# Gate and up of an expert as a 2 by 2 block product with seven block products for eight

## Chip, cores and metric

The kernel runs on one core of a Trainium2 chip. The metric is device time in microseconds (us) of one execution. "Expert phase" below means the part of the program in which the sixteen experts of the mixture of experts are computed one after another; "offset" is time counted from the first matmul of an expert.

## What is computed

The program has two layers: a convolution-like cross attention over 8 sequences of 256 tokens, then a mixture of experts with a shared expert. The change touches only the gated half of an expert:

```python
E, K, I = (16, 4, 352)          # experts, experts per token, hidden features
CAP = 256                       # token slots of an expert
xg = xpad[buf]                                            # (16, 256, 512)
gact = jax.nn.silu(jnp.einsum('ech,ehi->eci', xg, w_gate))
mid = gact * jnp.einsum('ech,ehi->eci', xg, w_up)
eout = jnp.einsum('eci,eih->ech', mid, w_down) * wbuf[..., None]
y = zeros.at[buf].add(eout)                               # scatter-add to tokens
```

For one expert, gate and up are two products of a 512 by 352 weight with 512 by 256 token columns, everything in float32.

## The kernel before

**Layout.** Features lie on the 128 partitions. The contraction of 512 is four chunks of 128. The 352 hidden features are two whole tiles of 128 (`NW = 2`) and a tail of 96. `w` holds gate and up of one expert as `[128, 2, 4, 352]`, `wd` the down weight, `xgT` the token columns as `[128, 4, 256]`, `mid` the result of gate times up.

**One expert** (loop at the end of the function). `gate_up` first does the tail: eight matmuls of 64 columns (L1046) and four of 128 (L1054, weights repacked into `wt` by `pack`), with two activations on L1063, one on L1067 and their multiplications by VectorE on L1064 and L1068. Then, for each of the two whole tiles, four matmuls for gate and four for up with 256 token columns (L1034), one Silu by ScalarE (L1041) and one multiplication by VectorE (L1042). After that `pack` copies the next expert's tail weights (ScalarE, L1017), `tokens` makes the next expert's `xgT` (VectorE: two column copies L1003, two transposes L404, both from the transferred `gb`), `find` computes the row numbers for the expert three ahead (sixteen small bf16 matmuls on L920 and VectorE's L928 to L943) and `gather` fetches those rows (GpSimd, indirect DMA, L977). `down` runs once for each half of the 256 tokens: three contraction tiles of 512 columns (L1080, the tail of `mid` first), a scaling by VectorE (L1088), and a scatter with addition into `out` by GpSimd (L1090, L1091). Then `compare` prepares the expert four ahead (VectorE, L907).

**Order.** The program order on every engine is the order in which the code is written; each engine works through its own list in order. Scatters of an expert wait for those of the expert before. The two scatters of expert 0 also wait for one another; from expert 1 on they do not.

**Transfers.** SyncE issues, for the expert three ahead, four weight loads (L859 to L864), then `slots` from the gathered rows (L989), then four loads of `gb` from `slots` (L992). Each of these waits in SyncE's list for the one before it to be issued, and `slots` and `gb` also for their data. There are three buffers for expert weights.

**Last experts.** Expert 15 has code of its own: it computes the two halves of the tokens one after the other, with matmuls of 128 token columns. There is nothing to gather or find for the last three.

**Room.** `xnT` holds the normalised tokens for the shared expert, 8192 floats a partition. Its last reader is the shared expert's last block, before expert 0. PSUM has two buffers of `ps_mm`, two of `ps_tr`, one of `ps_sm` and three of `ps_ex`; in the expert phase before the change only the last four are used.

Of the kernel before, what the change touches and what calls it, by code (L numbers as in the profile page):

```python
# [8 lines left out]
F32 = mybir.dt.float32  # L9
BF16 = mybir.dt.bfloat16  # L10
I32 = mybir.dt.int32
AF = mybir.ActivationFunctionType
# [8 lines left out]
P = 128  # L21
# [9 lines left out]
E, K, CAP, I, IS = 16, 4, 256, 352, 704  # L31
NSL = CAP // P
# [21 lines left out]
def ssm_attention__then__moe_kernel(  # L54
# [22 lines left out]
    nc = tc.nc  # L77
# [8 lines left out]
    ps_mm = ctx.enter_context(tc.tile_pool(name="ps_mm", bufs=2, space=PSUM))  # L86
    ps_tr = ctx.enter_context(tc.tile_pool(name="ps_tr", bufs=2, space=PSUM))
# [15 lines left out]
    xnT = keep.tile([P, NC, NT, P], F32, name="xnT")  # L103
# [156 lines left out]
    with ExitStack() as att:  # L260
# [591 lines left out]
    def load_expert(e):  # L852
# [92 lines left out]
    experts = {e: load_expert(e) for e in range(AHEAD)}  # L945
# [52 lines left out]
    def tokens(e):  # L998

        gb, g = moved.pop(e), gathered.pop(e)  # L1000
        wg = ffn.tile([P, NSL], F32, name="wg")
        for n in range(NSL):
            nc.vector.tensor_copy(wg[:, n : n + 1], g[:, n, L + e : L + e + 1])  # L1003
        xgT = ffn.tile([P, NC, CAP], F32, name="xgT")
        for n in range(NSL):
            transpose_blocks(xgT[:, :, n * P : (n + 1) * P], gb[:, n * NB : (n + 1) * NB])
        return xgT, wg

    NW, Q = I // P, P // 4
# [13 lines left out]
    def gate_up(xgT, mid, w, wt, cols, fs=(I // P, *range(I // P))):  # L1023

        halves = range(cols.start // P, cols.stop // P)
        for f in fs:
            pgu = ps_ex.tile([P, 2, CAP], F32, name="pgu", tag="ex")
            act = ffn.tile([P, CAP], F32, name="eact")  # L1030
            if f < NW:
                for k in range(2):
                    for c in range(NC):
                        nc.tensor.matmul(  # L1034
                            pgu[:, k, cols],
                            lhsT=w[:, k, c, f * P : (f + 1) * P],
                            rhs=xgT[:, c, cols],
                            start=(c == 0),
                            stop=(c == NC - 1),
                        )  # L1040
                nc.scalar.activation(act[:, cols], pgu[:, 0, cols], AF.Silu)  # L1041
                nc.vector.tensor_mul(mid[:, f, cols], act[:, cols], pgu[:, 1, cols])  # L1042
                continue
            for c in range(NC):
                for n in halves:
                    nc.tensor.matmul(  # L1046
                        pgu[2 * Q * n : 2 * Q * (n + 1), 1, 0:P],
                        lhsT=wt[:, c, P:],
                        rhs=xgT[:, c, n * P : (n + 1) * P],
                        start=(c == 0),  # L1050
                        stop=(c == NC - 1),
                    )
            for c in range(NC):
                nc.tensor.matmul(  # L1054
                    pgu[:, 0, cols],
                    lhsT=wt[:, c, 0:P],
                    rhs=xgT[:, c, cols],
                    start=(c == 0),
                    stop=(c == NC - 1),
                )  # L1060
            for n in halves:
                p, sl = 2 * Q * n, slice(n * P, (n + 1) * P)
                nc.scalar.activation(act[2 * Q : 3 * Q, sl], pgu[p : p + Q, 1, 0:P], AF.Silu)  # L1063
                nc.vector.tensor_mul(  # L1064
                    mid[2 * Q : 3 * Q, f, sl], act[2 * Q : 3 * Q, sl], pgu[p + Q : p + 2 * Q, 1, 0:P]
                )
            nc.scalar.activation(act[0 : 2 * Q, cols], pgu[0 : 2 * Q, 0, cols], AF.Silu)  # L1067
            nc.vector.tensor_mul(  # L1068
                mid[0 : 2 * Q, f, cols], act[0 : 2 * Q, cols], pgu[2 * Q : P, 0, cols]
            )  # L1070

    scattered = []
    between = route.tile([P, 1], F32, name="between")
    SYNC = mybir.DependencyInfo(mybir.DependencyClass.Sync, mybir.DependencyReason.DATA)

    def down(e, n, mid, wd, wg):
        po = ps_ex.tile([P, L], F32, name="eo", tag="ex")
        for k, f in enumerate((NW, *range(NW))):
            m = min(P, I - f * P)
            nc.tensor.matmul(  # L1080
                po,
                lhsT=mid[:m, f, n * P : (n + 1) * P],
                rhs=wd[:m, f, :],
                start=(k == 0),
                stop=(k == NW),
            )
        o = ffn.tile([P, L], F32, name="eo_sb", bufs=3)
        nc.vector.tensor_scalar_mul(o, po, wg[:, n : n + 1])  # L1088

        nc.gpsimd.memset(between, 0.0)  # L1090
        done = nc.gpsimd.indirect_dma_start(  # L1091
            out=out,
            out_offset=bass.IndirectOffsetOnAxis(ap=idx[:, e, n : n + 1], axis=0),
            in_=o,
            in_offset=None,
            compute_op=ALU.add,
        )


        done = done.ins  # L1100
        scattered.append(done)
        if e > 0:
            if n == 1:
                tc.declare_no_dep(done, scattered[2 * e], reason="other rows of out")
            for before in scattered[2 * (e - 1) : 2 * e]:
                tc.add_manual_dep(done, before.name, SYNC, reason="scatter")
# [6 lines left out]
    xgT_next = tokens(0)  # L1113
# [5 lines left out]
    for e in range(E):  # L1119
        w, wd = experts.pop(e)  # L1120
        wt = wt_next
        xgT, wg = xgT_next
        mid = ffn.tile([P, NI, CAP], F32, name="mid")
        if e + 1 < E:
            gate_up(xgT, mid, w, wt, slice(0, CAP))
            wt_next = pack(experts[e + 1][0])
            xgT_next = tokens(e + 1)
            if e + AHEAD < E:
                find(e + AHEAD, hots.pop(e + AHEAD))
                gathered[e + AHEAD] = gather(e + AHEAD)  # L1130
            for n in range(NSL):
                down(e, n, mid, wd, wg)
            if e + AHEAD + 1 < E:
                hots[e + AHEAD + 1] = compare(e + AHEAD + 1)
        else:

            gate_up(xgT, mid, w, wt, slice(0, P))
            gate_up(xgT, mid, w, wt, slice(P, CAP), (NW,))
            down(e, 0, mid, wd, wg)
            gate_up(xgT, mid, w, wt, slice(P, CAP), range(NW))  # L1140
            down(e, 1, mid, wd, wg)
        if e + AHEAD < E:
            experts[e + AHEAD] = load_expert(e + AHEAD)
            moved[e + AHEAD] = shuffle(gathered[e + AHEAD])
# [38 lines left out]
```

## Time and profile before

| | |
|---|---|
| time, median of 3 runs (lowest to highest) | 678.43 us (678.39 to 678.44) |
| profiled execution, its own time | 678.52 us |
| its span in the trace | 676.8 us |
| granted TensorE clock, mean | 0.995 |
| busy TensorE / VectorE / ScalarE / GpSimd | 654.2 / 385.8 / 184.2 / 320.2 us |
| expert 0 starts, expert 15 starts, last matmul ends | 419.3, 650.7, about 667 us |
| one expert, from 1 to 12 | 15.5 us |

Names: PE is TensorE's matmuls, PEld its weight loads, DVE VectorE, ACT ScalarE, POOL GpSimd, SP SyncE. A float32 matmul of the code appears in the trace as two instructions. Rows of the chain and of the timeline begin with start and length in us; `x32` counts merged instructions; in brackets stands the idle time before and what ended it. Rows of groups give count, busy us and the mean ns of one. Instructions of one engine overlap a little at their edges, so a recorded length can exceed the spacing between starts.

### The profile page before, as it was taken

The page shows a single profiled execution, that of the slowest core. Times are in us where ns is not written, and L with a number is a line of the kernel's source. Part 1 is how long each engine was busy: PE and PEld are TensorE (multiplying, and loading weights), DVE is VectorE, ACT ScalarE, POOL GpSimd, SP SyncE. Part 2 cuts the span into 40 slices and gives each one's busy share as a digit, 9 for nine tenths or more (in the row PEclk, how much of TensorE's full clock was granted, in tenths as well). Part 3 has the DMA queues.
Part 4 walks back from the last instruction along what each step waited for, and adds up shares of the span by engine and source line. Part 5 has one row for each costly group of instructions (what it writes and reads, how often), then busy time and mean ns, then how long its engine had stood idle before and what let it go on. Part 6 is the DMA issues. An engine that isn't in the chain of part 4 may idle for free.

```text
span 676.8 us, 9807 instructions
## 1 busy us (share of the span) xinstructions
PE 654.2 (97%) x3321; PEld 486.9 (72%) x3321; DVE 385.8 (57%) x932; ACT 184.2 (27%) x465; POOL 320.2 (47%) x509
## 2 busy tenths in 40 slices
PE   6899999998999999999999999999999999999994
PEld 5687877777867877876867685777776667777772
DVE  4956576878877776767536621444445545553231
ACT  2464533444342343313332010111121111111110
POOL 5677646877685777547120320243333444443111
PEclk9999999999999999999999999999999999999998
DMA  5793455555557536351008672588888889999822
GB/s 131 237 269 105 125 151 145 145 140 140 147 141 188 134 94 161 103 133 46 16 23 298 198 234 64 169 267 255 259 269 269 256 258 270 271 266 273 248 32 31
DMA packets 98439, 117.79 MB, mean 174 GB/s; under 512 B 11268, under 2 KB 64356, under 8 KB 98389
## 3 DMA queue, kind: packets, MB, share of 16 engines
q1 hardware_dynamic: 90932, 99.86, 48.9%
q0 software_dynamic: 7168, 17.04, 12.1%
q10 hardware_dynamic: 288, 0.26, 0.3%
q8 instruction: 26, 0.43, 0.3%
q14 instruction: 25, 0.20, 0.1%
HBM read 84.25 MB, written 32.88 MB: 173 GB/s over the span
## 4 chain that ended last, share of the span: by engine, by line
PE 85%; DVE 4%; DMA 3%; issue 2%; POOL 2%; ACT 2%; SPq 1%; POOLq 0%; DVEq 0%; ACTq 0%
PE sgu L168 20%; PE pgu L1034 15%; PE y L468 15%; PE eo L1080 12%; PE so L185 11%; PE pgu L1054 4%; PE pgu L1046 2%; PE sgt L154 2%; PE shared L468 2%; PE ip L920 1%; PE pt L529 1%; POOL kv L445 1%; DMA xs<-in_x 1%; DMA out<-eo_sb,idx 1%; DVE y L517 1%
## 5 line engine op out<-in xcount | busy, mean ns | idle before, releaser
L468 PE MATMUL y<-kv,toep 128*128 128x288 f32 x528 | 138.7, 407 | 4.8 <-DVE f L518 3.0
L468 PEld LDWEIGHTS y<-kv,toep 128*128 128x128 f32 x528 | 98.9, 190 | 35.4 <-issue 7.1
L977 POOL DMA_INDIRECT g<-xw_d,ido x32 | 34.9, 1092 | 170.8 <-DVE idx L943 132.3
L520 POOL TENSOR_TENSOR f<-f 128x256 f32<-128x256 f32 x60 | 43.8, 730 | 90.2 <-DVE f L518 85.0
L445 POOL TENSOR_TENSOR kv<-k 128x256 f32<-128x256 f32 x126 | 85.1, 707 | 0.0
L1091 POOL DMA_INDIRECT out<-eo_sb,idx x32 | 59.5, 1859 | 46.1 <-DVE eo_sb L1088 35.4
L168 PE MATMUL sgu<-xnT,swg 128*128 128x256 f32 (+1 forms) x400 | 78.1, 338 | 0.4 <-DVE tail L162 0.4
L1034 PE MATMUL pgu<-xgT,w 128*128 128x256 f32 (+1 forms) x384 | 78.2, 362 | 0.0
L168 PE MATMUL sgu<-xnT,swu 128*128 128x256 f32 (+1 forms) x400 | 77.9, 338 | 0.0
L1034 PEld LDWEIGHTS pgu<-xgT,w 128*128 128x128 f32 x384 | 68.2, 190 | 8.7 <-issue 0.5
L185 PE MATMUL so<-swd,smid 128*128 128x512 f32 x160 | 73.9, 593 | 0.0
L168 PEld LDWEIGHTS sgu<-xnT,swg 128*128 128x128 f32 x400 | 65.3, 191 | 7.9 <-DVE tail L162 0.6
L168 PEld LDWEIGHTS sgu<-xnT,swu 128*128 128x128 f32 x400 | 64.6, 191 | 6.3
L1080 PE MATMUL eo<-wd,mid 96*128 96x512 f32 (+1 forms) x132 | 59.4, 598 | 0.0
L1042 DVE TENSOR_TENSOR mid<-eact,pgu 128x256 f32<-128x256 f32 (+1 forms) x34 | 13.8, 406 | 77.6 <-ACT eact L1041 77.6
L491 DVE TENSOR_TENSOR y<-y,again 128x576 f32<-128x576 f32 x28 | 21.4, 766 | 57.8 <-PE y L468 48.1
L185 PEld LDWEIGHTS so<-swd,smid 128*128 128x128 f32 x160 | 29.9, 190 | 31.9 <-issue 30.4
L177 ACT ACTIVATE act<-sgu 128x256 f32<-128x256 f32 (+1 forms) x50 | 17.1, 341 | 121.6 <-PE sgu L168 121.6
L518 DVE TENSOR_TENSOR f<-y,z 128x512 f32<-128x512 f32 x64 | 44.3, 692 | 6.6 <-DVE y L517 0.5
L517 DVE TENSOR_TENSOR y<-y,q 128x512 f32<-128x512 f32 x64 | 44.8, 700 | 2.2
L1063 ACT ACTIVATE eact<-pgu 32x128 f32<-32x128 f32 x32 | 8.5, 267 | 129.0 <-PE pgu L1054 123.8
L1080 PEld LDWEIGHTS eo<-wd,mid 96*128 96x128 f32 (+1 forms) x132 | 24.1, 189 | 26.0 <-issue 23.5
(178 smaller groups left out, 928.2 us busy)
## 6 DMA issues: line engine op xcount, KB each, us to landing
toep<-win_d SPq DMA_DIRECT2D x28, 320.0 KB
slots<-g SPq DMA_DIRECT2D x16, 512.0 KB
gb<-slots SPq DMA_DIRECT2D x64, 128.0 KB
w<-in_L_ffn_w_gate SPq DMA_DIRECT2D x11, 704.0 KB
w<-in_L_ffn_w_up SPq DMA_DIRECT2D x11, 704.0 KB
got<-sent SPq DMA_DIRECT2D x26, 256.0 KB
wd<-in_L_ffn_w_down SPq DMA_DIRECT2D x11, 512.0 KB
xs<-in_x SPq DMA_DIRECT2D x16, 256.0 KB
```

The source lines that it names most:

```text
L168: nc.tensor.matmul(pgu[:, k, :], lhsT=sw[:, c, f * P : (f + 1) * P], rhs=toks[:, c, :], start=(c == 0), stop=(c == NC - 1),)
L185: nc.tensor.matmul(po, lhsT=m[:, i * P : (i + 1) * P], rhs=swd[:, (f - 1) % (NF + 1), :], start=(f == 0), stop=(f == NF),)
L445: (nc.vector if c in helped else nc.gpsimd).tensor_mul(kv[:, c, 0 : ND * HB].rearrange("p (d w) -> p d w", d=ND), kh[:, c, 0:HB].unsqueeze ...
L468: nc.tensor.matmul(out, lhsT=toep[:, m * P : (m + 1) * P], rhs=rhs, start=(n == 0), stop=(n == len(pairs) - 1),)
L517: nc.vector.tensor_mul(yd, yd, view(qq, 0, [[qc, 2], [B, ND], [1, HB]]))
L518: nc.vector.tensor_add(f, yd, z[:, :, :, BACK : BACK + HB])
L520: adder.tensor_add(f[:, :, 0:2, :], f[:, :, 0:2, :], f[:, :, 2:4, :])
L977: nc.gpsimd.indirect_dma_start(out=g[:, n, :], out_offset=None, in_=xw_d[:, :], in_offset=bass.IndirectOffsetOnAxis(ap=ido[:, e, n : n + 1 ...
L1034: nc.tensor.matmul(pgu[:, k, cols], lhsT=w[:, k, c, f * P : (f + 1) * P], rhs=xgT[:, c, cols], start=(c == 0), stop=(c == NC - 1),)
L1054: nc.tensor.matmul(pgu[:, 0, cols], lhsT=wt[:, c, 0:P], rhs=xgT[:, c, cols], start=(c == 0), stop=(c == NC - 1),)
L1080: nc.tensor.matmul(po, lhsT=mid[:m, f, n * P : (n + 1) * P], rhs=wd[:m, f, :], start=(k == 0), stop=(k == NW),)
L1091: done = nc.gpsimd.indirect_dma_start(out=out, out_offset=bass.IndirectOffsetOnAxis(ap=idx[:, e, n : n + 1], axis=0), in_=o, in_offset=Non ...
```

## The change

For experts 1 to 14 the two whole feature tiles of gate and up become one product of 2 by 2 blocks: rows gate and up (256 features each), contraction halves (two chunks each), columns the two halves of the tokens (128 each). Seven block products are done in place of eight, in the variant with four sums on each side. `weight_sums` lets GpSimd compute four sums of `[128, 2, 256]` for the next expert's weights, at the head of an expert's work. `token_sums` lets VectorE compute four sums of `[128, 2, 128]` for the next expert's tokens, after `tokens`. `strassen` does the seven products (four matmuls of 128 token columns each) in four PSUM tiles, three of which take two products one on top of the other. ScalarE copies out two of them between, VectorE adds the rest and multiplies. The sums and intermediate results lie in the old `xnT`. The tail tile stays as it was and comes first. `down` takes the second half of the tokens first. Experts 0 and 15 keep the old code.

```diff
+    F = NW * P
+    free = xnT.rearrange("p c n q -> p (c n q)")
+
+    def spare(at, n):
+        return free[:, at : at + n]
+
+    def blocks_of(w):
+        return [[w[:, m, 2 * k : 2 * k + 2, 0:F] for k in range(2)] for m in range(2)]
+
+    def weight_sums(e, w):
+        (a11, a12), (a21, a22) = blocks_of(w)
+        sums = [
+            spare((e % 2 * 4 + i) * 2 * F, 2 * F).rearrange("p (c f) -> p c f", c=2)
+            for i in range(4)
+        ]
+        nc.gpsimd.tensor_add(sums[0], a21, a22)
+        nc.gpsimd.tensor_sub(sums[1], sums[0], a11)
+        nc.gpsimd.tensor_sub(sums[2], a11, a21)
+        nc.gpsimd.tensor_sub(sums[3], a12, sums[1])
+        return sums
+
+    def token_sums(e, xgT):
+        (b11, b12), (b21, b22) = [
+            [xgT[:, 2 * k : 2 * k + 2, n * P : (n + 1) * P] for n in range(2)] for k in range(2)
+        ]
...
+        nc.vector.tensor_sub(sums[0], b12, b11)
+        nc.vector.tensor_sub(sums[1], b22, sums[0])
+        nc.vector.tensor_sub(sums[2], b22, b12)
+        nc.vector.tensor_sub(sums[3], b21, sums[1])
+        return sums
+
+    def strassen(xgT, mid, w, s, t):
...
+        ps = [
+            pool.tile([P, NW, P], F32, name=f"gu{i}", tag=tag)
+            for i, (pool, tag) in enumerate(((ps_mm, "mm"), (ps_mm, "mm"), (ps_tr, "pt"), (ps_tr, "pt")))
+        ]
+        begun = set()
+
+        def product(i, a, b):
+            for f in range(NW):
+                for c in range(2):
+                    nc.tensor.matmul(
+                        ps[i][:, f, :],
+                        lhsT=a[:, c, f * P : (f + 1) * P],
+                        rhs=b[:, c, :],
+                        start=(i not in begun),
+                        stop=(c == 1),
+                        skip_group_check=True,
+                    )
+                    begun.add(i)
...
+        product(0, a11, b11)
+        nc.scalar.copy(p1, ps[0])
+        product(1, s[1], t[1])
+        nc.vector.tensor_add(u2, ps[1], p1)
+        product(2, s[0], t[0])
+        nc.scalar.copy(p5, ps[2])
+        product(0, a12, b21)
+        nc.scalar.activation(act0, ps[0], AF.Silu)
+        product(2, s[3], b22)
+        nc.vector.tensor_add(u2, ps[2], u2)
+        nc.scalar.activation(act1, u2, AF.Silu)
+        product(1, s[2], t[2])
+        nc.vector.tensor_add(u3, ps[1], p1)
+        nc.vector.tensor_add(p5, u3, p5)
+        nc.vector.tensor_mul(mid[:, 0:NW, P : 2 * P], act1, p5)
+        product(3, a22, t[3])
+        nc.vector.tensor_add(u3, ps[3], u3)
+        nc.vector.tensor_mul(mid[:, 0:NW, 0:P], act0, u3)
...
         if e > 0:
-            if n == 1:
+            if len(scattered) % 2 == 0:
                 tc.declare_no_dep(done, scattered[2 * e], reason="other rows of out")
...
+        if e + 2 < E:
+            s_next = weight_sums(e + 1, experts[e + 1][0])
         if e + 1 < E:
-            gate_up(xgT, mid, w, wt, slice(0, CAP))
+            if e == 0:
+                gate_up(xgT, mid, w, wt, slice(0, CAP))
+            else:
+                gate_up(xgT, mid, w, wt, slice(0, CAP), (NW,))
+                strassen(xgT, mid, w, sums, token_sums_now)
             wt_next = pack(experts[e + 1][0])
             xgT_next = tokens(e + 1)
+            if e + 2 < E:
+                sums, token_sums_now = s_next, token_sums(e + 1, xgT_next[0])
             if e + AHEAD < E:
                 find(e + AHEAD, hots.pop(e + AHEAD))
                 gathered[e + AHEAD] = gather(e + AHEAD)
-            for n in range(NSL):
+            for n in reversed(range(NSL)):
                 down(e, n, mid, wd, wg)
```

More of the change, by code (lines that the diff above doesn't have):

```diff
@@ new lines, in token_sums @@
+    def token_sums(e, xgT):
+        (b11, b12), (b21, b22) = [
+            [xgT[:, 2 * k : 2 * k + 2, n * P : (n + 1) * P] for n in range(2)] for k in range(2)
+        ]
+        at = 16 * F
+        sums = [
+            spare(at + (e % 2 * 4 + i) * 2 * P, 2 * P).rearrange("p (c q) -> p c q", c=2)
+            for i in range(4)
+        ]
[4 more added lines that the diff above has]
+        return sums
@@ new lines, in strassen, with place @@
+    def strassen(xgT, mid, w, s, t):
+        (a11, a12), (a21, a22) = blocks_of(w)
+        (b11, b12), (b21, b22) = [
+            [xgT[:, 2 * k : 2 * k + 2, n * P : (n + 1) * P] for n in range(2)] for k in range(2)
+        ]
+        ps = [
+            pool.tile([P, NW, P], F32, name=f"gu{i}", tag=tag)
+            for i, (pool, tag) in enumerate(((ps_mm, "mm"), (ps_mm, "mm"), (ps_tr, "pt"), (ps_tr, "pt")))
+        ]
+        begun = set()
[11 more added lines that the diff above has]
+                    begun.add(i)
+        def place(i):
+            return spare(16 * F + 16 * P + i * F, F).rearrange("p (f q) -> p f q", f=NW)
+        p1, p5, u2, u3, act0, act1 = (place(i) for i in range(6))
+        product(0, a11, b11)
[16 more added lines that the diff above has]
+        nc.vector.tensor_mul(mid[:, 0:NW, 0:P], act0, u3)
```

## The prediction

> **What bounds it now.** I began with the page's slices, to see which engine is full in the expert phase (slices 25 to 39, from 423 us).
>
> ```profile
> PE   6899999998999999999999999999999999999994
> POOL 5677646877685777547120320243333444443111
> DMA  5793455555557536351008672588888889999822
> ```
>
> TensorE is full to the end, the transfers nearly so, GpSimd has room. The chain that ended last, in order of time, gives one expert (here the eighth) link by link:
>
> ```profile
> 527.79 1.02 PE pgu L1046 x16
> 528.82 1.92 PE pgu L1054 x8
> 530.74 6.91 PE pgu L1034 x32
> 538.03 5.26 PE eo L1080 x12
> 543.29 1.02 PE pgu L1046 x16
> ```
>
> 15.5 us an expert, all TensorE; no wait of TensorE stands in it. So each us taken from L1034 counts fourteen times (experts 1 to 14), as long as nothing else needs more than the new period. The windows by expert say how near the others are:
>
> ```profile
> 589.70:605.20 15.50, 15.50 (x85) 11.04 (x84) 7.63 (x19) 2.49 (x7) 6.22 (x7) 1.00 0.97 277
> ```
>
> VectorE 7.63, GpSimd 6.22 of 15.5; transfers 97% of the time, clock 1.00.
>
> **What TensorE saves.** Seven products of four matmuls are 28 matmuls, 56 instructions of 128 columns, for 32 of 256 columns. Expert 15 already runs the same weights against 128 columns, so the timeline of the weight loads has both paces:
>
> ```profile
> 530.37 6.88 PEld L1034 LDWEIGHTS pgu<-xgT,w 128*128 128x128 f32 x32
> ...
> 661.01 3.54 PEld L1034 LDWEIGHTS pgu<-xgT,w 128*128 128x128 f32 x31 [0.24 <-issue]
> ```
>
> Less the last load's own 0.19: 6.69 over 31 steps is 0.216, 3.35 over 30 is 0.112. Old 32 x 0.216 = 6.91, new 56 x 0.112 = 6.25: 0.65 an expert, 9.2 over fourteen; period 14.84. The half-wide instruction costs 3% more than half, no more.
>
> [...]
>
> **What GpSimd adds.** Its additions in the attention layer:
>
> ```profile
> L445 POOL TENSOR_TENSOR kv<-k 128x256 f32<-128x256 f32 x126 | 85.1, 707 | 0.0
> L451 POOL TENSOR_TENSOR kv<-kv 128x288 f32<-128x288 f32 x28 | 22.4, 799 | 0.0
> L443 POOL TENSOR_TENSOR kv<-k 128x128 f32<-128x128 f32 x32 | 14.7, 458 | 2.2 <-ACT k L418 2.2
> ```
>
> From 128 to 256 elements 1.95 ns an element, to 288 2.1; for 512 I extend to 1.2 to 1.3 us. Four: 5.0 us, GpSimd 11.2 of 14.84: not full. Its order is gathers, scatters, sums:
>
> ```profile
> 540.84 1.02 POOL L977 DMA_INDIRECT g<-xw_d,ido  x1 [8.60 <-DVE idx L943]
> ...
> 545.37 2.36 POOL L1091 DMA_INDIRECT out<-eo_sb,idx  x1 [0.19 <-issue]
> ```
>
> First gather at offset 13.1 (expert began 527.73), second scatter done 6.2 to 6.9 later. The gather waits for VectorE's `idx`, which token sums (below) push to about 14.5, so sums start at 14.5 + 6.2 to 6.9 - 14.84 = 5.9 to 6.6 and last until 11 to 12.5. The sums are due in the next expert's second product, 6 us later, and the next gather at 14.5: their result is hidden. Weights for them landed long before (`pack` reads them without wait).
>
> **What VectorE adds, and the lock.** Products end at offsets 2.85 + 0.893 k: 3.74, 4.64, 5.53, 6.42, 7.32, 8.21, 9.10. Other engines follow 0.20 behind (TensorE's L1034 ends 537.49, ACT starts 537.69). A 256-element VectorE instruction takes 0.42 (L1042), a dependent one starts 0.04 later, a ScalarE copy takes 0.38. After the sixth product: u3 8.41 to 8.83, p5 to 9.29, `mid` of the second half ready 9.75. `down` takes the tail first and needs `mid` at 9.10 + 0.40 (find) + 0.86 = 10.36. Slack 0.6. The last u3 and product end 10.55, due 2.6 later. Copies p1 and p5 have 0.4 to 0.6 slack. So all of it is hidden, if VectorE runs at its own pace. Two views say that it won't:
>
> ```profile
> 15.22 0.72 DVE L520 TENSOR_TENSOR f<-f 128x256 f32<-128x256 f32 x1
> 15.97 0.67 DVE L521 TENSOR_TENSOR oT<-f 128x128 f32<-128x128 f32 x1
> ...
> 32.28 0.42 DVE L520 TENSOR_TENSOR f<-f 128x256 f32<-128x256 f32 x1
> 32.74 0.29 DVE L521 TENSOR_TENSOR oT<-f 128x128 f32<-128x128 f32 x1
> ```
>
> ```profile
> 14.95 1.54 POOL L445 TENSOR_TENSOR kv<-k 128x256 f32<-128x256 f32 x2
> ```
>
> The same VectorE instructions take 0.30 and 0.38 longer while GpSimd adds (at 19.28 and 19.92 by 0.19 and 0.39; mean 0.31). Both read two SBUF operands. L517, with one operand in PSUM, took 698 to 700 ns in all 64 cases, GpSimd busy or not. New instructions with two SBUF operands in the time of the sums are three: p5 and both multiplications.
>
> [...]
>
> Price of a wait: below, 0.31 as in the rows; above, 0.31 + 0.55, all that a 512 sum is longer. I scale with the length, 0.31 x 1.25/0.70 = 0.56; the third multiplication lies at the sums' end, so 2.5 waits, 1.4 us.
>
> What that does is a loop through VectorE, from the start of the fourth product: three products and handover 2.88; u3, p5, product, u3, product 2.14; columns and transposes 1.34; four token sums 1.72; find 1.0; two scalings 1.3; compare 2.24; the tail's hand-to-hand chain with ScalarE (L1064, L1063, L1064, L1067) 1.34; copy of p1 0.38, which lets the next fourth product start. 14.34 without waits, under TensorE's 14.84; with 1.4, 15.74. VectorE becomes the bound at 0.25 over the old 15.49. Thirteen experts have sums beside them (1 to 13): +3.3; expert 14 has none: -0.65. 678.52 + 2.6 = **681.1** (median 0.09 below the profiled time, ignored). Three waits at 0.31 give 15.28, -3.4, 675.1; 2.5 at 0.86 give 16.5, +12.5, 691.
>
> The rest costs nothing: reversed `down` and the new parity keep the same dependencies, PSUM tiles were idle, GpSimd's late first sums (expert 0's second scatter was issued at 442.5) delay one gather by 2 us, which the transfers hold.
>
> **Rivals.**
>
> *No lock that matters* (faster): the sums fall beside instructions that don't contend. TensorE's 14.84 stands: 669.3. For it: the loop needs waits of 1.15 in total to reach 15.49, three of 0.38; the rows' mean is 0.31. Against: the sums are longer than those of the rows. Here transfers take part back: expert 15's tokens landed at 643 (DMA share 0.38 in 642 to 643, then 0.00), and VectorE needs them 1.5 before its start, 650.74 - 9.2 - 1.5 = 640.0. If they come no earlier, 3 us: 672.3. I take 670.5.
>
> *The transfers take over* (slower): the gather moves from offset 13.1 to about 16, and SyncE's list (`slots` waits for gather, `gb` for `slots`, next weights behind) moves with it, at 97% DMA. 3 us later is 646 for expert 15, due 649.2: it fits by 3. At 0.5 us more for each of twelve turns it's 3 us over: with the lock, 684 to 687.
>
> *The change doesn't do what it says*: if ordering is kept on the whole old `xnT`, the second product waits for sums of the next expert, written ahead of it: from 3.74 to about 12, 14 x 8 = 112 us slower. Against: before, VectorE writes some columns of `xnT` while TensorE reads others.
>
> **Chances.** Lock 0.58 (slower 0.40, same 0.10, faster 0.08), no lock 0.27 (faster 0.25, same 0.02), transfers 0.10, whole-tile order or a GpSimd beyond its period 0.05. Faster 0.33, same 0.12, slower 0.55; 0.2% (1.4 us) is what a measurement of this kernel can tell from no change. The range must take in most of the no-lock case and the lock up to about 0.8 a wait: 670 to 689; the lock case alone 675 to 691.
>
> **What would show it.** L1034's place taken by 56 instructions at 0.112; p5 and the multiplications at 0.7 to 1.3 instead of 0.42; sums of 1.2 to 1.3 us at offsets 6 to 12; TensorE waiting ahead of the fourth product or of `down`'s second tile, released by ACT or DVE; period 15.3 to 16.5. Three short multiplications and 14.84 mean that I was wrong on the lock; waits on `xgT` mean transfers.

## The result, and the profile after

The changed kernel takes 693.66 us (median of four runs, 692.95 to 694.32) where the kernel before takes 678.43 (678.39 to 678.56). The ratio is 1.0225, with a 95% interval from 1.0213 to 1.0237. The profiled execution took 692.95, its span is 691.2; the span before was 676.8, so 14.4 us have to be found. The change makes the kernel slower, through the mechanism that was forecast, and by 15.2 us instead of 2.7. Ratios, here and below, leave out executions more than 1.5% above the shortest of the same kernel.

The slices of the page come first: TensorE still looks full, at a steady 8 to 9 tenths, GpSimd has gone from 3 or 4 tenths to 7, the transfers are a little less busy.

```profile
PE   7899999998999999999999999989999999999894
POOL 5677645786775567654110530687777777777511
DMA  5884456655465555330039542788888889888922
```

One expert (expert 8, counted from 0) in the chain that ended last, in order of time; each row is start, length, engine, result, line:

```profile
551.23 1.02 PE pgu L1046 x16
552.25 1.92 PE pgu L1054 x8
554.17 2.68 PE gu L1133 x24
556.85 0.28 issue
557.13 2.96 PE gu L1133 x24
...
560.11 0.44 DVE xnT L1159
...
560.57 1.17 DVE xnT L1160
...
561.83 1.31 DVE mid L1161
...
563.18 4.56 PE eo L1170 x10
567.75 1.02 PE pgu L1046 x16
```

An expert now takes 16.52 us (551.23 to 567.75) instead of 15.5. TensorE's part up to the end of the sixth product is short, as the change meant. Then the chain leaves TensorE: u3 (L1159), the sum p5 (L1160) and the multiplication into `mid` (L1161) stand in it for 3 us, and `down`'s second tile (L1170) starts only after them. The two instructions that last 1.17 and 1.31 are the same size as the one that lasts 0.44.

What makes them long is seen when VectorE and GpSimd are laid side by side, in the timeline of that expert:

```profile
559.59 1.84 POOL L1096 TENSOR_TENSOR xnT<-w 128x512 f32<-128x512 f32 x1
560.11 0.42 DVE L1159 TENSOR_TENSOR xnT<-gu,xnT 128x256 f32<-128x256 f32 x1 [0.41 <-PE gu L1133]
560.57 1.15 DVE L1160 TENSOR_TENSOR xnT<-xnT 128x256 f32<-128x256 f32 x1
561.51 1.33 POOL L1097 TENSOR_TENSOR xnT<-xnT,w 128x512 f32<-128x512 f32 x1
561.83 1.30 DVE L1161 TENSOR_TENSOR mid<-xnT 128x256 f32<-128x256 f32 x1
562.81 1.45 POOL L1098 TENSOR_TENSOR xnT<-w 128x512 f32<-128x512 f32 x1
563.05 0.41 DVE L1163 TENSOR_TENSOR xnT<-gu,xnT 128x256 f32<-128x256 f32 x1
563.50 1.05 DVE L1164 TENSOR_TENSOR mid<-xnT 128x256 f32<-128x256 f32 x1
...
564.23 1.46 POOL L1099 TENSOR_TENSOR xnT<-w,xnT 128x512 f32<-128x512 f32 x1
```

The first sum of GpSimd ends at 561.43, p5 at 561.72. The second sum ends at 562.84, the multiplication at 563.13. The third ends at 564.26, the last multiplication at 564.55. Each VectorE instruction with two operands in SBUF (`xnT<-xnT`, `mid<-xnT`) ends 0.29 us after the sum beside it; u3 (`xnT<-gu,xnT`, one operand in PSUM) keeps its 0.41 to 0.42 in the midst of the sums. The groups by form show the means over the experts:

```profile
L1161 DVE TENSOR_TENSOR mid<-xnT 128x256 f32<-128x256 f32 x13 | 18.2, 1397 | 1.4
L1160 DVE TENSOR_TENSOR xnT<-xnT 128x256 f32<-128x256 f32 x14 | 14.9, 1067 | 0.5
L1164 DVE TENSOR_TENSOR mid<-xnT 128x256 f32<-128x256 f32 x13 | 13.0, 999 | 0.5
L1159 DVE TENSOR_TENSOR xnT<-gu,xnT 128x256 f32<-128x256 f32 x14 | 5.9, 424 | 5.4 <-PE gu L1133 5.4
```

These means mix in the experts at both ends (expert 1 has one multiplication of 2.58 and no wait of p5; expert 14 has no sums). In experts 2 to 12 the three always take 1.14 to 1.18, 1.30, and 1.04 or 1.05. Less 0.42 that is 0.73, 0.88 and 0.63 of waiting, 2.2 us an expert. With the prediction's loop through VectorE, 14.34, that makes 16.58; measured are 16.52 to 16.56 in experts 3 to 12.

The sum over the experts: from the starts of L1046 in both traces, expert 1 costs 1.04 more than before, expert 2 1.88, experts 3 to 12 1.03 each, expert 13 2.0, expert 14 0.63 less. That is 14.6 for the 14.4 of the spans.

### The profile page after: what moved, and what is told of

Its sections match the earlier page's. It is cut to its first block, busy times and chain, and to the rows that moved or that the text cites. A ratio compares the mean times of both kernels' runs of the same rounds, so it can differ in the third digit from the quotient of the medians.

```text
span 691.2 us, 10764 instructions
## 1 busy us (share of the span) xinstructions
PE 652.2 (94%) x3657; PEld 490.5 (71%) x3657; DVE 464.4 (67%) x1058; ACT 192.3 (28%) x493; POOL 411.6 (60%) x565
## 3 DMA queue, kind: packets, MB, share of 16 engines
q0 software_dynamic: 7168, 17.04, 12.2%
## 4 chain that ended last, share of the span: by engine, by line
PE 73%; DVE 14%; issue 4%; DMA 3%; POOL 2%; ACT 2%; SPq 1%; POOLq 0%; DVEq 0%; ACTq 0%
PE sgu L168 19%; PE y L468 14%; PE so L185 11%; PE gu L1133 10%; PE eo L1170 7%; PE pgu L1054 3%; DVE mid L1161 3%; DVE xnT L1160 2%; PE sgt L154 2%; PE shared L468 2%; PE pgu L1046 2%; DVE hot L907 1%; PE pgu L1034 1%; PE pt L529 1%; DVE xnT L1159 1%
## 5 line engine op out<-in xcount | busy, mean ns | idle before, releaser
L977 POOL DMA_INDIRECT g<-xw_d,ido x32 | 58.3, 1822 | 95.5 <-DVE idx L943 54.8
L520 POOL TENSOR_TENSOR f<-f 128x256 f32<-128x256 f32 x60 | 43.7, 729 | 90.5 <-DVE f L518 85.2
L1181 POOL DMA_INDIRECT out<-eo_sb,idx x32 | 52.2, 1631 | 37.3 <-DVE eo_sb L1178 28.3
L1170 PE MATMUL eo<-wd,mid 96*128 96x512 f32 (+1 forms) x132 | 61.8, 605 | 9.1 <-DVE mid L1161 9.1
L1170 PEld LDWEIGHTS eo<-wd,mid 96*128 96x128 f32 (+1 forms) x132 | 23.3, 189 | 38.2 <-issue 19.2
L1133 PE MATMUL gu<-xnT 128*128 128x128 f32 x336 | 42.1, 275 | 0.0
L1133 PEld LDWEIGHTS gu<-xnT 128*128 128x128 f32 x336 | 39.8, 192 | 0.0
L179 DVE TENSOR_TENSOR smid<-act,sgu 128x256 f32<-128x256 f32 (+1 forms) x50 | 18.0, 361 | 28.8 <-ACT act L177 28.1
```

Of the source, the lines that this page charges most:

```text
L520: adder.tensor_add(f[:, :, 0:2, :], f[:, :, 0:2, :], f[:, :, 2:4, :])
L977: nc.gpsimd.indirect_dma_start(out=g[:, n, :], out_offset=None, in_=xw_d[:, :], in_offset=bass.IndirectOffsetOnAxis(ap=ido[:, e, n : n + 1 ...
L1133: nc.tensor.matmul(ps[i][:, f, :], lhsT=a[:, c, f * P : (f + 1) * P], rhs=b[:, c, :], start=(i not in begun), stop=(c == 1), skip_group_ch ...
L1170: nc.tensor.matmul(po, lhsT=mid[:m, f, n * P : (n + 1) * P], rhs=wd[:m, f, :], start=(k == 0), stop=(k == NW),)
L1181: done = nc.gpsimd.indirect_dma_start(out=out, out_offset=bass.IndirectOffsetOnAxis(ap=idx[:, e, n : n + 1], axis=0), in_=o, in_offset=Non ...
```

## The experiments

The theory, taken from the rows above (ends 0.29 after the sum's end, 0.42 with an operand in PSUM), and called the lock: a VectorE instruction that reads two operands from SBUF (the memory in which this kernel's tiles lie; TensorE's results lie in PSUM) and a sum of GpSimd exclude one another for a whole instruction, and the expert's period is TensorE's 14.84 or VectorE's loop of 14.34 plus all such waits, whichever is longer. The rivals: the later gathers make the transfers the bound; or the half-wide matmuls or GpSimd's length of work set the period, and the long VectorE instructions are only a symptom.

**Without the sums.**

```diff
-        nc.gpsimd.tensor_add(sums[0], a21, a22)
-        nc.gpsimd.tensor_sub(sums[1], sums[0], a11)
-        nc.gpsimd.tensor_sub(sums[2], a11, a21)
-        nc.gpsimd.tensor_sub(sums[3], a12, sums[1])
```

> The change without GpSimd's four sums of weights (the products read whatever lies in that room, so the output of experts 1 to 14 is not the reference's). Theory A, the lock: the 15.2 us come from GpSimd's sums, which make the three VectorE instructions with two SBUF operands (L1160, L1161, L1164) 1.07, 1.40 and 1.00 us long where 0.42 was expected. Without sums they take 0.42, TensorE's 14.84 us an expert is the bound, 669 to 672 us. Theory B, VectorE's own added work (the token sums, the additions of the products) fills its loop whatever GpSimd does: the period stays near 16.5 and the time near 693. Theory C, the transfers take over: TensorE waits for xgT, 684 or more.

Measured: 674.11 us (671.14 to 675.36, three runs), ratio to before 0.9929 [0.9903, 0.9954]. In the profiled run (671.14) twelve of experts 1 to 14 take 14.85 or less, expert 9 takes 15.18 and expert 11 16.20. The timeline, with the helper's lines four lower, shows p5 and the two multiplications at their own length:

```profile
562.74 0.42 DVE L1156 TENSOR_TENSOR xnT<-xnT 128x256 f32<-128x256 f32 x1
563.27 0.42 DVE L1157 TENSOR_TENSOR mid<-xnT 128x256 f32<-128x256 f32 x1
...
564.06 0.43 DVE L1160 TENSOR_TENSOR mid<-xnT 128x256 f32<-128x256 f32 x1
...
581.25 1.30 DVE L404 STREAM_TRANSPOSE xgT<-gb 128x512 f32<-128x512 f32 x2 [1.79 <-DMA gb<-slots]
```

So the half-wide products do give the 14.84, and the sums cost all that is lost. The last row is the second finding: at this pace the tokens of the next expert come late (`gb<-slots`, six waits of 7.9 us in all in the expert phase). The spread of the three runs, 671 to 675, I put down to the transfers; only the shortest of them has a trace.

**The sums alone, in the kernel before.** Their results are not used.

```diff
+        if e + 2 < E:
+            weight_sums(e + 1, experts[e + 1][0])
         if e + 1 < E:
             gate_up(xgT, mid, w, wt, slice(0, CAP))
```

> The kernel before, with GpSimd's sums of weights added at the head of experts 0 to 13 and used by nobody. Theory A: before the change VectorE's instructions beside the sums have one operand in PSUM (L1042, L1064, L1068), so they keep 0.42 and 0.29 us and the time stays within 1 us of 678.4; a sum that meets no VectorE instruction with two SBUF operands takes 1.2 to 1.3 us. A rival, that any GpSimd addition slows any VectorE instruction (shared bandwidth, by operands in SBUF at all): L1042 gets longer than 0.5 us. Its result is not on the chain's critical step by more than 0.4 us (slack of tail and find), so the time would still stay under 684, but the rows would show it.

Measured: 678.27 (eight runs, 678.18 to 678.50), ratio 0.9999 [0.9989, 1.001]; every expert keeps the period that it had before. Two rows of its groups, a sum and the old multiplication, and two of its timeline, where such a multiplication stands beside the sums:

```profile
L1094 POOL TENSOR_TENSOR xnT<-w 128x512 f32<-128x512 f32 x8 | 10.2, 1278 | 0.0
L1042 DVE TENSOR_TENSOR mid<-eact,pgu 128x256 f32<-128x256 f32 x28 | 11.8, 421 | 67.1 <-ACT eact L1041 67.1
```

```profile
548.99 1.27 POOL L1093 TENSOR_TENSOR xnT<-xnT,w 128x512 f32<-128x512 f32 x1
...
550.09 0.42 DVE L1042 TENSOR_TENSOR mid<-eact,pgu 128x256 f32<-128x256 f32 x1 [1.86 <-ACT eact L1041]
```

A sum on its own is 1.28 us, and 421 ns is the old multiplication's length without any sums, though fourteen of them run beside a sum: `pgu` lies in PSUM. GpSimd's work and its room in time cost nothing here; what the change adds is VectorE instructions that it disturbs.

**Half as long sums.** Eight instructions of 256 elements instead of four of 512.

```diff
-        nc.gpsimd.tensor_add(sums[0], a21, a22)
-        nc.gpsimd.tensor_sub(sums[1], sums[0], a11)
-        nc.gpsimd.tensor_sub(sums[2], a11, a21)
-        nc.gpsimd.tensor_sub(sums[3], a12, sums[1])
+        for c in range(2):
+            s = [x[:, c, :] for x in sums]
+            b11, b12, b21, b22 = (x[:, c, :] for x in (a11, a12, a21, a22))
+            nc.gpsimd.tensor_add(s[0], b21, b22)
+            nc.gpsimd.tensor_sub(s[1], s[0], b11)
+            nc.gpsimd.tensor_sub(s[2], b11, b21)
+            nc.gpsimd.tensor_sub(s[3], b12, s[1])
```

> The change with each of GpSimd's sums in two instructions of 256 elements (one for each chunk), eight an expert in place of four; the same additions and the same result. Theory A with a lock that is held for a GpSimd instruction: a VectorE instruction waits for what is left of one short instruction, as in the attention layer (0.2 to 0.4 us each), so the three waits fall from 2.2 to about 1.0 us, the period to about 15.4 to 15.7 and the time to 678 to 683, although GpSimd works longer in all (8 x 0.70 = 5.6 at its own pace). A rival, sharing of bandwidth: what a VectorE instruction loses depends on how busy GpSimd is beside it, not on the length of one instruction; the rows stay near 1.0 to 1.4 us and the time near 693.

Measured: 689.23 (two runs), ratio 1.016 [1.014, 1.0181], period 16.41: my 678 to 683 missed. The timeline (lines three higher than in the changed kernel) says why:

```profile
560.10 0.61 DVE L1163 TENSOR_TENSOR xnT<-xnT 128x256 f32<-128x256 f32 x1
560.81 0.76 DVE L1164 TENSOR_TENSOR mid<-xnT 128x256 f32<-128x256 f32 x1
561.94 0.51 DVE L1167 TENSOR_TENSOR mid<-xnT 128x256 f32<-128x256 f32 x1
...
563.83 1.00 DVE L1115 TENSOR_TENSOR xnT<-xgT 128x256 f32<-128x256 f32 x1
564.86 0.83 DVE L1116 TENSOR_TENSOR xnT<-xgT,xnT 128x256 f32<-128x256 f32 x1
565.61 0.94 DVE L1117 TENSOR_TENSOR xnT<-xgT 128x256 f32<-128x256 f32 x1
```

The first three rows are p5 and the multiplications: their waits fell to 0.19, 0.34 and 0.09. So here the waits are shorter beside the shorter sums: 0.62 in all for 2.2. But eight sums last longer, and the token sums (L1115 to L1117) now wait 0.58, 0.41 and 0.52, 1.5 in all. In both places together 2.1; 14.34 + 2.1 is 16.4. I had counted the waits of three instructions, where the four token sums read two SBUF operands too and belong to the loop.

**The sums moved to VectorE.** `nc.gpsimd` becomes `nc.vector` in the four lines.

> The change with the four sums of weights on VectorE in place of GpSimd. No wait for GpSimd is left, but VectorE's loop gets four instructions of 512 elements, 0.6 to 0.7 us each as L1178 and the additions of the attention layer. Theory A with the loop through VectorE of 14.3 us plus what is added: 14.3 + 2.6 = 16.9 to 17.1 a period, 697 to 702. If VectorE's length were not the bound (GpSimd's own time, or its order): 671 to 680.

Measured: 693.02 (two runs), ratio 1.0216 [1.0198, 1.0234], period 16.84. No wait is left (L1160, L1161 and L1164 have a mean of 425 ns), but four sums of 0.65 each stand in the loop: 14.34 + 2.6 = 16.9. The time came out 4 below what I had expected, since only twelve experts (1 to 12) pay for it. Done by VectorE itself, the sums cost the same as waiting for GpSimd (693.02 for 693.66).

**Without the token sums.** The four subtractions in `token_sums` are dropped; they take 1.72 of VectorE's loop.

> The change without VectorE's four token sums (the products read whatever lies there, so experts 1 to 14 are not the reference's); GpSimd's sums stay. It takes 1.72 us out of VectorE's loop and leaves the three waits. Theory A, by the loop: 16.53 - 1.72 = 14.8, so the loop is no longer the bound, but TensorE still waits directly for the second half of mid (ready at 9.75 plus about 1.6 of waits, due 10.36), period 15.3 to 15.9, 676 to 684. If the loop is not the bound but only that direct wait, nothing changes: 16.5 and 693.

Measured: 677.89 (eight runs), ratio 0.9996 [0.9986, 1.0006], period 15.31 to 15.37. In these experts p5 and the first multiplication still wait 0.09 and 0.89. The loop is now under TensorE's period, and only the part of these waits beyond the slack of `down`'s second tile shows: 15.34 - 14.84 = 0.5 of the 0.98, a slack of 0.48. Expert 1 took 19.14: TensorE stood 2.34 ahead of `down`'s second tile, and the ten instructions behind the wait then took 6.26, where in the changed kernel's chain above they take 4.56 (see the last section).

**One operand of each from PSUM.** ScalarE writes the Silu back into PSUM, and p5 becomes two additions that each read a PSUM tile. GpSimd's work is untouched.

```diff
-        nc.scalar.copy(p5, ps[2])
+        nc.vector.tensor_add(p5, ps[2], p1)
...
-        nc.scalar.activation(act0, ps[0], AF.Silu)
+        nc.scalar.activation(ps[0], ps[0], AF.Silu)
...
-        nc.scalar.activation(act1, u2, AF.Silu)
+        nc.scalar.activation(ps[2], u2, AF.Silu)
         product(1, s[2], t[2])
+        nc.vector.tensor_add(p5, ps[1], p5)
+        nc.vector.tensor_mul(mid[:, 0:NW, P : 2 * P], ps[2], p5)
         nc.vector.tensor_add(u3, ps[1], p1)
-        nc.vector.tensor_add(p5, u3, p5)
-        nc.vector.tensor_mul(mid[:, 0:NW, P : 2 * P], act1, p5)
...
-        nc.vector.tensor_mul(mid[:, 0:NW, 0:P], act0, u3)
+        nc.vector.tensor_mul(mid[:, 0:NW, 0:P], ps[0], u3)
```

> The change with one operand of each VectorE instruction of the products in PSUM: ScalarE writes both Silu results into PSUM, and the product that had been copied out by ScalarE is added by VectorE straight from PSUM, so none of VectorE's eight instructions there reads two SBUF operands. The sums on GpSimd stay as they are. Theory A: each of the eight takes 0.42 us, the loop through VectorE is back to about 14.3, TensorE's 14.84 the bound: 669 to 673 us, faster than both. Theory B: one VectorE instruction more, so 693 or above. If the transfers are next, TensorE or VectorE waits for gb in the last experts and the time is 672 to 676.

Measured: 679.92 (ten runs), ratio 1.0021 [1.0011, 1.003], period mostly 15.48. Most of the loss is gone, but the 669 to 673 missed. The timeline:

```profile
570.50 0.42 DVE L1160 TENSOR_TENSOR mid<-gu,xnT 128x256 f32<-128x256 f32 x1
570.85 0.41 DVE L1161 TENSOR_TENSOR xnT<-gu,xnT 128x256 f32<-128x256 f32 x1
571.36 0.42 DVE L1163 TENSOR_TENSOR xnT<-gu,xnT 128x256 f32<-128x256 f32 x1
571.82 0.42 DVE L1164 TENSOR_TENSOR mid<-gu,xnT 128x256 f32<-128x256 f32 x1
...
574.07 1.38 DVE L1113 TENSOR_TENSOR xnT<-xgT,xnT 128x256 f32<-128x256 f32 x1
```

The four instructions after the products run at 0.42 while GpSimd adds (its sums last from 569.29 to 575.2 here); here the operands that are read make the difference, not the size of the work: p5 and both multiplications, of the same size, took 1.15, 1.30 and 1.05 in the changed kernel. But now VectorE is early enough that its token sums, which still read two SBUF operands, meet the last weight sum: L1113 waits 0.96. 14.34 + 0.96 is 15.3 for the 15.48 measured; 0.2 I cannot place.

**The sums earlier.** The four sums are written behind the gathers and ahead of the scatters, for the expert two ahead, so that they run at offset 4 to 10 of the next expert. `if e == 0` keeps the first set.

```diff
-        if e + 2 < E:
-            s_next = weight_sums(e + 1, experts[e + 1][0])
+        if e == 0:
+            s_next = weight_sums(1, experts[1][0])
...
                 gathered[e + AHEAD] = gather(e + AHEAD)
+            if e + 3 < E:
+                s_next = weight_sums(e + 2, experts[e + 2][0])
```

> The change with nothing but the order in GpSimd's list altered: sums behind the gathers and ahead of the scatters. Operands as in the change (three instructions with two SBUF operands). Theory A: what counts is whether a sum runs beside L1160, L1161 and L1164 (offset 8.9 to 10.6). Sums at offset 4 to 10 meet the first one or two of them, at most 1.5 us of waits in place of 2.2, and no token sum: period 14.84 to 15.6, 672 to 681. A rival, that the sums cost what they cost wherever they stand: near 693.

Measured: 675.0 (four runs, 672.65 to 678.53), ratio 0.9939 [0.9924, 0.9953]: moving the sums is enough to make the change faster than the kernel before in the median, inside the range expected; the profiled run, 678.53, is the slowest of the four. In it the first multiplication, L1161, has a mean of 425 ns, p5 still 559. Periods of experts 1 to 12 lie between 14.84 and 18.62; in the four from 16.5 up `compare` (L907) comes late and meets the sums, as in the next kernel.

**Both: PSUM operands and early sums.**

> Both at once: the products' VectorE instructions with one operand in PSUM as in the run before, and GpSimd's sums one place earlier in its list, behind the gathers and ahead of the scatters of the same expert (so for the expert two ahead). In the run with PSUM operands alone the products were free of waits, but the period was 15.48 us: a token sum (L1113) took 1.38 instead of 0.42 behind the last of GpSimd's sums, which ended at offset 14.5, and expert 2 lost 4.3 us behind expert 0's second scatter. Theory A: sums now run at offset 4 to 10, where VectorE has no instruction with two SBUF operands; the token sums take 0.42, the period is 14.84 and the time that of the change without sums, 671 to 675 (transfers of the last experts take 2 to 5 us of the 9.2), faster than both kernels. A rival, that VectorE's loop is over TensorE's period even without any wait on GpSimd (one instruction more than the change has): period 15.3 to 15.5, 676 to 680.

Measured: 676.91 (twelve runs, 671.1 to 680.05), ratio 0.9975 [0.9955, 0.9995], above the 671 to 675 expected. Ten of the fourteen experts take 14.85 or less, but experts 4, 7, 9 and 12 take 16.74 to 16.81. The timeline of expert 9:

```profile
558.40 0.75 DVE L1178 TENSOR_SCALAR eo_sb<-eo,wg 128x512 f32<-128x512 f32 x1 [0.68 <-DMA out<-eo_sb,idx]
559.07 3.73 DVE L907 TENSOR_TENSOR hot<-pos,slot_f 128x2048 bf16<-128x2048 f32 x1
559.36 1.27 POOL L1096 TENSOR_TENSOR xnT<-w 128x512 f32<-128x512 f32 x1
560.72 3.20 POOL L1097 TENSOR_TENSOR xnT<-xnT,w 128x512 f32<-128x512 f32 x1
```

In such an expert the scaling L1178 waited for a buffer that an old scatter still read. `compare` (L907), which also reads two SBUF operands, then came together with the first sum: it took 3.73 instead of 2.28, the first sum its usual 1.27, and the second sum behind `compare` 3.20. The exclusion works in this direction too. The recorded starts alone do not tell which of the two is served first: here L907 starts 0.29 ahead of the sum and still waits for it. In this kernel it waited with leads of up to 0.61 and was served first with leads of 0.70 and more.

**Four buffers for `eo_sb`.** The line is the same in both kernels; one has the early sums alone, the other also the PSUM operands.

```diff
-        o = ffn.tile([P, L], F32, name="eo_sb", bufs=3)
+        o = ffn.tile([P, L], F32, name="eo_sb", bufs=4)
```

> The change with early sums and a fourth eo_sb buffer, operands as in the change. Without that buffer it took 675.0 us, with experts of 14.84 and others of 15.0 to 18.6. Theory A: the comparison always ahead of the sums; then sums run from about offset 4 to 9.5 and meet the first of the three multiplications for 0.4 us at most, inside the 0.6 us of slack: 14.84 to 14.9 a period, 669 to 675, the same as with PSUM operands within 2 us. If the operands matter in this order too: 2 to 6 us slower than the run with PSUM operands.

> PSUM operands and early sums as in the run with both, and a fourth buffer for the scaled outputs (eo_sb). In that run most experts took 14.84 us, but four took 16.75: there the second scaling (L1178) waited for a scatter to release its buffer, the comparison (L907, two SBUF operands) came after the first of GpSimd's sums had begun, and took 3.73 instead of 2.28. Theory A, the lock with its order of arrival: with the fourth buffer the scaling doesn't wait, the comparison comes first, every expert takes 14.84, and the time is 669 to 674 with what the transfers cost. A rival, that scatters or transfers are late in themselves and the buffer only shows it: the wait moves to xgT or to a later scatter, 675 to 679 as before.

With early sums alone: 677.61 (twelve runs, 670.68 to 679.54), ratio 0.9971 [0.9944, 0.9997]; the expected 669 to 675 missed, and the fourth buffer shows no gain over the 675.0 without it. In its profiled run (671.75) one instruction of the three still meets the last sum; p5 takes 1.08 to 1.09, and the period is 15.03 instead of 14.84. A wait of 0.66 thus costs 0.2, so the slack of `down`'s second tile is 0.46 by this kernel.

With both: 674.92 (six runs, 668.83 to 683.15), ratio 0.9916 [0.9886, 0.9947]; two of the six took 681.81 and 683.15. The 669 to 674 expected was just missed. In the profiled run (674.85) `compare` and the products' instructions no longer wait for GpSimd, as the groups show, and experts 1 to 11 take 14.84 or 14.85:

```profile
L907 DVE TENSOR_TENSOR hot<-pos,slot_f 128x2048 bf16<-128x2048 f32 x12 | 27.4, 2284 | 0.0
L1160 DVE TENSOR_TENSOR mid<-gu,xnT 128x256 f32<-128x256 f32 x14 | 6.0, 425 | 1.5
```

Then experts 12 to 14 take 15.80, 17.05 and 16.53, and this row of its waits says for what:

```profile
DVE xgT L404 <- DMA gb<-slots: 9.7, 4, 5.4
```

Four waits, 9.7 in all, 5.4 the longest. This kernel has the shortest single run of all, four of its six runs are faster than both kernels of the case, and two are slower than the one before. The profiled run is limited by when the transfers bring the tokens: experts 12 to 14 lose 5.8 us there (14.84, 14.37 and 14.37 without a wait). What made the two long runs longer, no trace shows.

**Tokens ahead of the weights.** In the kernel with both and four buffers, SyncE issues `slots` and `gb` of the expert three ahead first, its weights after them.

```diff
-            experts[e + AHEAD] = load_expert(e + AHEAD)
             moved[e + AHEAD] = shuffle(gathered[e + AHEAD])
+            experts[e + AHEAD] = load_expert(e + AHEAD)
```

> The early sums, the PSUM operand and four buffers stay; at the end of an expert SyncE issues slots and gb of the expert three ahead before that expert's weights, not behind them. In the kernel without this, slots waited up to 11.8 us for its data behind 1.9 MB of weights, and experts 12 to 14 took 15.80, 17.05 and 16.53 us. Theory (the order in SyncE's list makes the tokens late, the sum of the bytes does not): gb is there in time for every expert, all of experts 1 to 14 take 14.84, time 668.5 to 671, and the spread between runs shrinks. Rival (the bytes themselves fill the transfers, 97 to 99% busy): the wait moves from the tokens to the weights, shown by pack or by the tail's matmuls L1046 waiting on the load of w, and the time stays at 673 to 678.

Measured: 693.95 (six runs, 690.73 to 698.61), ratio 1.0229 [1.0196, 1.0261]. Both expected times missed. The wait went to the weights, as the rival said (`pack`, L1017, now waits for them, 16.5 in seven times), but GpSimd waits longest:

```profile
POOL xnT L1096 <- DMA w<-in_L_ffn_w_up: 27.8, 6, 5.8
```

The early sums need the weights of the expert two ahead; with these behind the tokens the first sum waited up to 5.8, with the scatters and the next gathers behind it in GpSimd's list, and experts took up to 19.75. So the weights have no slack to give the tokens in this arrangement. Whether another order, or only fewer bytes, would give 14.84 in every expert stays open.

## Why the prediction was wrong

**Right: what TensorE saves.** 56 instructions at 0.112 and a period of 14.84 were measured to the hundredth as soon as nothing else was longer (the kernel without sums, and the last one but one). Expert 14, which has no sums beside it, was taken at -0.65 and gave -0.63.

**Right: the lock and the loop.** The three instructions named are those that wait (0.73, 0.88 and 0.63), and u3 with its PSUM operand does not (0.41 to 0.42). The loop of 14.34 plus waits gives the measured period of three kernels within 0.1: 16.58 for 16.53, 16.4 for 16.41, 16.9 for 16.84; with the PSUM operands it is 0.2 short. TensorE waits where it was said, ahead of `down`'s second tile, and for 0.28 ahead of the fourth product; the chain shows both.

**Wrong: the size of the waits, 1.4 taken and 2.2 measured.** This is the step that failed, and nearly all of the miss: 0.8 in thirteen experts is 10.4, and experts 2 and 13 cost 0.85 and 1.0 more than the others, 12.2 in all; the profiled execution lies 11.9 over the forecast (692.95 - 681.1). In expert 2 the first token sum also waited, 1.28 instead of 0.42. In expert 13 TensorE stood 0.62 ahead of its fifth product, for ScalarE's copy L1152, and 1.55 ahead of `down`'s second tile; what held up that copy is not shown.

I took 0.56 a wait, by scaling the mean wait of the attention layer's rows, 0.31, in proportion to the length of the sum. But in these rows a wait is no share of the sum's length. It is what is left of the sum when VectorE's instruction starts, less 0.13 to 0.15. The attention layer's rows already said so. The two GpSimd additions that the prediction shows merged, one by one:

```profile
14.95 0.70 POOL L445 TENSOR_TENSOR kv<-k 128x256 f32<-128x256 f32 x1
```

```profile
15.61 0.89 POOL L445 TENSOR_TENSOR kv<-k 128x256 f32<-128x256 f32 x1
```

L520 starts at 15.22, when 0.43 of the first is left, and waits 0.30; L521 starts at 15.97, when 0.53 of the second is left, and waits 0.38. In the changed kernel p5 starts with 0.86 of its sum left and waits 0.73, the first multiplication with 1.01 and waits 0.88, the last with 0.76 and waits 0.63; the first multiplication beside half sums starts with 0.49 left and waits 0.34. L520 and the first multiplication start at nearly the same place, 0.27 and 0.32 after the start of the instruction beside them. The sum beside the first multiplication is 0.63 longer (1.33 for 0.70) and the wait 0.58 (0.88 for 0.30). So nearly all that the sum is longer goes into the wait. That was the upper price of the prediction, 0.31 + 0.55 = 0.86, and the first multiplication measured it; 2.5 waits at this price would have given 691. Of the 0.8, about 0.5 is the size of the first two waits (1.61 for 1.12) and 0.35 the third, of which I took half.

So in these rows a VectorE instruction with two SBUF operands waits until the sum beside it is nearly over: each of the three, 0.42 on its own, ends 0.29 after its sum.

**Wrong: when the sums run.** I put them at offsets 5.9 to 6.6, ending by 12.5, and so took half of the last wait. They start at 8.4 (559.59 less 551.23) and end at 14.5, on top of all three instructions. I had the gather's second instruction at 0.97, from rows where it ran alone. In the changed kernel `compare` runs beside it; two experts of the changed kernel, the first with `compare`, the second (expert 13) without:

```profile
553.26 3.06 POOL L977 DMA_INDIRECT g<-xw_d,ido  x1 [0.30 <-issue]
```

```profile
635.91 0.97 POOL L977 DMA_INDIRECT g<-xw_d,ido  x1 [0.30 <-issue]
```

The offset was out by 1.8 to 2.5. These rows account for 1.3 of it: the second gather is 2.1 longer, and the second scatter, which no longer runs beside `compare`, 0.8 shorter (1.57). Another 1.1 is the first gather, which starts 0.7 into the next expert (551.95 less 551.23) where I had it 0.3 ahead of that. The trace of before had the hint: its second scatter took 2.36 beside L907 where the one before it took 1.61, and I read 2.36 as that instruction's own length. The sums themselves were priced well: 1.2 to 1.3 forecast, 1.28 measured alone, 1.33 to 1.46 where VectorE's instructions come between (the first sum's 1.84 overlaps the record of the scatter ahead of it, which ends at 560.12, by 0.53).

**Wrong, with little effect: slack 0.6.** Two kernels give 0.46 and 0.48.

**The rivals.** "No lock" was given 670.5, with the transfers taking back about one us. Where the lock was taken away (without the sums, and with PSUM operands, early sums and four buffers), single runs of 669 to 671 do occur, but the medians are 674 to 675, about 5 over the 669.3 that TensorE alone would give. In the one run of them with such a time and a trace, 674.85, late tokens cost 5.8, more than the 3 that I had as the transfers' worst. Their takeover, which I placed in the slower rival, is real, only it acts at 14.84 and not at 16.5: at the changed kernel's pace they had time enough (share 0.88 in the window of one expert, where it was 0.97 before), and nothing that makes `xgT` waits for `gb` in its trace. Whole-tile ordering did not happen.

## What to carry to other kernels

Before giving GpSimd elementwise work on SBUF, list the VectorE instructions that will run beside it, mark those with two SBUF operands, and price each at what will be left of the GpSimd instruction when it starts (waits of 0.63 to 0.88 us here, beside sums of 1.3 to 1.8). Here the wait beside the longer instruction was longer by nearly the whole extra length, not in proportion to it: 0.30 beside 0.70, 0.88 beside 1.33. Then move the work in time, or put one operand into PSUM: here either one took back all or nearly all of the loss (675.0 and 679.92, for 693.66 with it and 678.43 before). And when an engine's period is about to shrink, look at what the transfers were doing under the old one: at 97% busy there may be little to win behind it (here about 5 of the 9.2 us that TensorE would have saved were lost to it).

## What the runs showed of the hardware

- An indirect gather's issue on GpSimd took 0.97 alone and 3.06 beside VectorE's L907 (2.28, two SBUF operands). In the expert shown it ends at 556.32, 0.85 after L907 (553.19 + 2.28 = 555.47). In this trace the gather as a whole took 2.09 longer; which part of it waited is not shown.
- In the kernel with PSUM operands and early sums the exclusion went both ways: L907 took 3.73 instead of 2.28 where a sum (1.27) was served first, and the next sum then took 3.20 behind L907.
- A stall of TensorE of 2.37 us was followed by a granted clock of 0.50. In the kernel with PSUM operands, TensorE stood 2.37 ahead of expert 2's fourth product; the window up to that product (454 to 457.5) shows a granted clock of 1.00, the windows after it 0.64 and 0.50; the columns are length, busy time and count of TensorE, weight loads, VectorE, ScalarE, GpSimd, then clock, share of the transfers, GB/s:

```profile
457.50:459.00 1.50, 1.50 (x8) 1.50 (x9) 0.89 (x3) 0.00 (x0) 1.31 (x3) 0.64 0.52 168
459.00:460.70 1.70, 1.70 (x9) 1.70 (x9) 0.00 (x0) 0.37 (x1) 1.70 (x2) 0.50 0.95 89
```

  A group of eight matmuls took 1.91 instead of 1.06, and the expert 19.11 where most take 15.48. The next windows show 0.85 (460.7 to 462.8) and 1.00 (to 468.5). From these clocks I estimate 1.7 us lost, as much as 3.4 us at half clock. The late product so cost more here than its own lateness. In the expert phase of five other kernels TensorE was slower too behind idle stretches of 1.89 to 3.02 us: groups of eight took up to 1.91 with early sums, 1.92 with half sums and 2.08 with tokens ahead of the weights (1.06 elsewhere), L1054 3.59 instead of 1.99 with both and four buffers, `down`'s ten 6.26 without the token sums. The mean granted clock of these five runs is 0.985 to 0.994, of the four changed kernels without such a stretch (no sums, sums on VectorE, both with three buffers, early sums with four) 0.995 to 0.997. It did not follow stretches of 1.90 and 2.38 in the kernel with tokens ahead of the weights, nor any of up to 1.74 (eleven of 1.72 to 1.74 with the sums on VectorE), so the length of one stretch alone does not decide.
